# Neighbour lists from eight-column codes on TensorE, and layer 1 summed before its product

## The chip, the cores and the metric

One Trainium2 chip, one of its cores. A core has five engines that run side by side, each with its own queue, in order: TensorE (PE; its weight loads are listed as PEld), VectorE (DVE), ScalarE (ACT), GpSimd (POOL) and SyncE (SP, which only issues DMAs here). The metric is the device time of one launch in microseconds (us); lower is better. The figure of a kernel is the median of its runs.

## The reference, cut to what matters

16 graphs of 1024 nodes with 64 features go through four layers; each normalises x, applies relu, and adds its result to x. The sparse adjacency `adj` (with self loops, weights from 0.05 to 1) is the same in all of them. Layer 0 is a gated update on `A @ m`, layer 1 a normalised propagation, layer 3 a mean. Layer 2 needs the neighbours themselves: it takes out up to two neighbours of a node with many, in both directions, and then sums three quantiles of each feature over the neighbours that are left.

```python
# layer 1
norm_adj = d_inv_sqrt[:, :, None] * adj * d_inv_sqrt[:, None, :]
transformed = jnp.einsum('bnf,fu->bnu', node_features, kernel)
out = jnp.einsum('bnm,bmu->bnu', norm_adj, transformed)
# layer 2
m = nb.sum(-1)
rank = jnp.cumsum(nb, axis=-1) - 1
skip = jnp.where(m > T_THRESH, (m + K_DIL - 1) // K_DIL, 1)
do_dil = (skip > 1) & mask
removed = nb & do_dil[..., None] & ((rank + 1) % skip[..., None] == 0)
rem = removed | jnp.swapaxes(removed, 1, 2)
adj_d = jnp.where(rem, 0.0, adj_)
# then: sort the features of the neighbours of each node, channel by channel,
# and add their 0.25, 0.5 and 0.75 quantiles with weights 0.25, 0.5, 0.25
```

## The kernel before

Nodes are sorted by degree. The 128 of highest degree are the heavy rows (tile 0, in classes of capacity `HEAVY`), the other 896 the light ones (tiles 1 to 7, `LIGHT`). For each row the kernel makes a list of its neighbours, GpSimd gathers their features from a table in DRAM, and VectorE sorts them with min/max networks. The code is a set of Python generators, one for each stage and graph:

- `load` reads 128 rows of `adj` at a time (`a`), transposes them on TensorE and stores them as `adjT`; ScalarE sums the rows (`rs`).
- `ranks` makes `kx`, the column number plus one where there is a neighbour and 0 elsewhere, in fp16, stores it in DRAM as `kd`, and counts degrees with a Sign and an accumulator. Comparing the degrees gives each node its place (`sg`, `posi`). One-hot products `oh` then carry id, degree and mask of each node (`trip`) into rank order (`info`, `idn`).
- `lists` gathers the first 256 rows of `kd` in rank order (`ks2`), scans them for the rank of each neighbour, finds the one or two to be removed (`cut`), and writes zeros into `kd` at those places and their mirror images with eight scatters. It then gathers all rows again, tile by tile (`ks`), and takes the largest eight entries with MAX8, strikes them out with MATCH_REPLACE8, and repeats (`rounds`). The longest rows are cut into eight segments on the way, through `seg` and `cl` in DRAM. The lists become the indices `idxL` and `idxH`, the quantile weights `wl` and `w`.
- `dense01` is layers 0 and 1, and stores the table `tab`. `propagated` streams `adjT` through TensorE as `am`, row block by row block. Biases enter as one-row fp32 products.
- `gather_heavy` and `gather_light` issue one indirect DMA for each list position (`gh`, `s`); heavy rows pass through TensorE to put channels on partitions (`hb`). `sort_heavy`, `sort_light` and `sum_light` sort and sum; the light sorts are called 0 (tiles 1 to 3, tile `s0`) and 1 (tiles 4 to 7, `s1`). Each `s` has two buffers, `gh` six.
- `dense23` gathers the sums back to node order (`zz` from `agg`) and does the rest of layer 2 and layer 3.

The order of all instructions is fixed before the launch. The class `Order` keeps a clock for each engine from assumed durations (`Engine.duration`), and at each `yield` runs the stage that can start first; ties go to rear, sums, mid, list, rank, load, gath, sort in that order, so sorts fill what the others leave. `after(...)` holds a stage back until another has been emitted. A graph loads once the graph before has been loaded and ranked, and the graph five before has been finished (`DEPTH`). Every engine call passes through one helper line, L357, so the profile tells instructions apart by their tiles.

Of the kernel before, what the change touches and what calls it, by code (L numbers as in the profile page):

```python
# [9 lines left out]
F32 = mybir.dt.float32  # L10
# [8 lines left out]
P = 128  # L19
EPS = 1e-5  # L20
STRIP = 2
DEPTH = 5
TAUS = (0.25, 0.5, 0.75)
# [3 lines left out]
NOWHERE = 4194304.0  # L27
# [26 lines left out]
SEG_A, SEG_B, SEG_C = 26, 14, 16  # L54
USED = {1: 13, 2: 10, 3: 9, 4: 7, 5: 6, 6: 5, 7: 4}
# [123 lines left out]
class Order:  # L179
# [52 lines left out]
    def put(self, engine, us, outs, ins, landing=None, scatter=False, tail=0.0):  # L232
# [7 lines left out]
        for x in outs:  # L240
            t = max(t, self.used.get(x, 0.0), self.ready.get(x, 0.0) if scatter else 0.0)
            p = self.follows.pop(x, None)
            if p is not None:
                t = max(t, self.used.get(p, 0.0) + 0.05, self.ready.get(p, 0.0) + 0.05)
# [46 lines left out]
class Engine:  # L291
# [5 lines left out]
    def duration(self, name, outs, ins):  # L297
# [17 lines left out]
        if self.letter == "T":  # L315
            n = 1
            for _, c in list(outs[0].ap)[1:]:
                n *= c
            if name == "transpose":
                return (0.06 if ins[0].shape[0] <= 64 else 0.215), 0.17  # L320
            if two_bytes(ins[0]):
                return 0.04 + n / 2600, 0.2
            return max(0.02 + n / 510, 0.43 if ins[0].shape[1] > 64 else 0.0), 0.25
# [39 lines left out]
def kernel(  # L363
# [48 lines left out]
    onesh = const.tile([P, N], F16, name="onesh")  # L412
# [42 lines left out]
    biases = const.tile([65, 512], F32, name="biases")  # L455
    ones3 = const.tile([65, P], F32, name="ones3")
    nc.vector.memset(ones3, 1.0)
    for i, (src, n) in enumerate(((b2, H), (c2, H), (bg, 4 * H))):
        nc.sync.dma_start(biases[32 * i : 32 * i + 1, 0:n], src)
        o = biases[32 * i : 32 * i + 1, :]  # L460
        for k in range(1, 512 // n):
            nc.vector.tensor_copy(o[:, k * n : (k + 1) * n], o[:, 0:n])

    def bias(i):
        return ones3[32 * i : 32 * i + 1, :], biases[32 * i : 32 * i + 1, :]
# [7 lines left out]
    def lists_for_all():  # L473
# [9 lines left out]
        ps1 = pool("ps1", 6, space=bass.MemoryType.PSUM)  # L483
        ps2 = pool("ps2", 1, space=bass.MemoryType.PSUM)
# [29 lines left out]
        zero1 = lc.tile([P, 1], F16, name="zero1")  # L514
        nc.vector.memset(zero1, 0.0)
# [32 lines left out]
        for i in range(DEPTH):  # L548
            d = {
                "kd": dram.tile([N, N], F16, name=f"kd{i}"),  # L550
                "seg": dram.tile([32, N], F16, name=f"seg{i}"),
# [29 lines left out]
        def load(b, S):  # L581
# [8 lines left out]
            S["rs"] = rs = st.tile([P, NT], F32, name="rs")  # L590
            S["a"] = []
            for t in range(NT):
                a = ap_.tile([P, N], F32, name="a", bufs=2)
                S_.dma_start(a, adj[b, t * P : (t + 1) * P, :])
                S["a"].append(a)
                yield f"a{b}.{t}"
# [3 lines left out]
                for m in range(0, NT, 4):  # L600
# [6 lines left out]
                    ps1.close(pt)  # L607
                if t % STRIP == STRIP - 1:
                    yield "S", strip
                    S_.dma_start(  # L610
                        d["adjT"].rearrange("(m p) n -> p m n", p=P)[:, :, (t + 1 - STRIP) * P : (t + 1) * P], strip
                    )
                junk = ap_.tile([P, N], BF16, name="junk", bufs=1)
                A.activation(junk, a, AF.Copy, accum_out=rs[:, t : t + 1])
                yield after(f"b{b}.{max(0, t - 1)}")
            yield "V", rs
            V.tensor_scalar(rs, rs, 1.0, None, ALU.add)

        def ranks(b, S):

            d = D[b % DEPTH]
            yield after(f"a{b}.0")
# [3 lines left out]
            deg = ap_.tile([P, NT], F32, name="deg", bufs=2)  # L626
            for t in range(NT):
                yield after(f"a{b}.{t}")
                a = S["a"][t]
                yield "V", a  # L630
                kx = ap_.tile([P, N], F16, name="kx", bufs=2)
                V.scalar_tensor_tensor(kx, a, 0.0, iota1, ALU.is_gt, ALU.mult)
                dg = kx[:, t * P : (t + 1) * P]
                V.tensor_mul(dg, dg, offdiagh)
                yield "S", kx
                S_.dma_start(d["kd"][t * P : (t + 1) * P, :], kx)
                yield "A", kx
                junk = ap_.tile([P, N], BF16, name="junk", bufs=1)
                A.activation(junk, kx, AF.Sign, accum_out=deg[:, t : t + 1])
                yield f"b{b}.{t}"  # L640
            yield "V", deg
            trip = ap_.tile([P, NT, 3], F16, name="trip", bufs=2)
            V.tensor_scalar(trip[:, :, 0], nid, 1.0, None, ALU.add)
            V.tensor_copy(trip[:, :, 1], deg)
            V.tensor_copy(trip[:, :, 2], nm)
# [30 lines left out]

            pm = yield from bank2()
            for t in range(NT):
                yield ("V",)
                oh = ap_.tile([P, N], F16, name="oh", tag="nb", bufs=2)  # L680
                V.tensor_scalar(oh, iota1, pos1[:, t : t + 1], None, ALU.is_equal)
                yield "T", oh
                for i in range(NH):
                    sl = slice(i * 512, (i + 1) * 512)
                    T.matmul(pm[0:3, sl], trip[:, t, :], oh[:, sl], start=(t == 0), stop=(t == NT - 1))
            yield "A", pm
            byr = ap_.tile([3, N], F16, name="byr", tag="nb", bufs=2)
            A.copy(byr, pm[0:3, :])
            ps2.close(pm)
            yield "T", byr  # L690
            pb = yield from bank(F16)
            for t in range(NT):
                T.transpose(pb[:, 4 * t : 4 * t + 3], byr[:, t * P : (t + 1) * P], identh[0:3, 0:3])
            yield "V", pb
            info = ap_.tile([P, NT, 3], F32, name="info", bufs=2)
            V.tensor_copy(info, pb[:, 0 : 4 * NT].rearrange("p (t c) -> p t c", c=4)[:, :, 0:3])
            ps1.close(pb)
            idn = ap_.tile([P, NT], I32, name="idn", bufs=2)
            V.tensor_scalar(idn, info[:, :, 0], -1.0, None, ALU.add)
            S["info"], S["idn"] = info, idn  # L700

        def lists(b, S):
            d = D[b % DEPTH]
            yield after(f"rank{b}")
            info, idn = S["info"], S["idn"]

            def ranked(dst, t):
                G_.indirect_dma_start(
                    out=dst, out_offset=None, in_=d["kd"][:, :],
                    in_offset=bass.IndirectOffsetOnAxis(ap=idn[:, t : t + 1], axis=0),  # L710
                )
# [3 lines left out]
            ks2 = ap_.tile([P, 2, N], F16, name="ks2", tag="ks2")  # L715
            yield "P", idn, d["kd"]
            for t in range(2):
                ranked(ks2[:, t, :], t)
            yield "V", ks2
            inf = info[:, 0:2, :]  # L720
            half_i = ap_.tile([P, 2], I32, name="half_i", bufs=2)
            V.tensor_scalar(half_i, inf[:, :, 1], 1.0, None, ALU.add)
            V.tensor_scalar(half_i, half_i, 1, None, ALU.logical_shift_right)
            r12 = ap_.tile([P, 2, 2], F32, name="r12", bufs=2)
            V.tensor_copy(r12[:, 0, :], half_i)
            dil = ap_.tile([P, 2], F32, name="dil", bufs=2)
            V.scalar_tensor_tensor(dil, inf[:, :, 1], T_THRESH, inf[:, :, 2], ALU.is_gt, ALU.mult)
            V.tensor_mul(r12[:, 0, :], r12[:, 0, :], dil)
            V.tensor_scalar(r12[:, 1, :], r12[:, 0, :], 2.0, None, ALU.mult)
            cut = ap_.tile([P, 2, 2], F32, name="cut", bufs=2)  # L730
            for t in range(2):
                yield ("V",)
                nbk = ap_.tile([P, N], F16, name="nb", tag="nb", bufs=2)
                V.tensor_scalar(nbk, ks2[:, t, :], 1.0, None, ALU.min)
                rank = ap_.tile([P, N], F16, name="rank", tag="rank")
                V.tensor_tensor_scan(rank, onesh, nbk, 0.0, ALU.mult, ALU.add)
                for i in range(2):
                    e = ap_.tile([P, N], F16, name="e", tag="mr")
                    V.scalar_tensor_tensor(
                        e, rank, r12[:, i, t : t + 1], ks2[:, t, :], ALU.is_equal, ALU.mult,  # L740
                        accum_out=cut[:, t, i : i + 1],
                    )
                    yield ("V",)
            offi = ap_.tile([P, 2, 2, 2], I32, name="offi", bufs=2)
            none = ap_.tile([P, 2, 2], F32, name="none", bufs=2)
            V.tensor_scalar(none, cut, 0.0, NOWHERE, ALU.is_equal, ALU.mult)
            own = ap_.tile([P, 2, 2], F32, name="own", bufs=2)
            V.scalar_tensor_tensor(own, inf[:, :, 0:1].to_broadcast([P, 2, 2]), float(N), cut, ALU.mult, ALU.add)
            V.scalar_tensor_tensor(offi[:, 0], own, -float(N + 1), none, ALU.add, ALU.add)
            V.scalar_tensor_tensor(own, cut, float(N), inf[:, :, 0:1].to_broadcast([P, 2, 2]), ALU.mult, ALU.add)  # L750
            V.scalar_tensor_tensor(offi[:, 1], own, -float(N + 1), none, ALU.add, ALU.add)
            for w in range(2):
                for t in range(2):
                    for i in range(2):
                        yield "P", offi, d["kd"]
                        G_.indirect_dma_start(
                            out=d["kd"].rearrange("n (w o) -> (n w) o", o=1),
# [1093 lines left out]
```

## Time and profile before

| | us |
|---|---|
| median of 3 runs | 3383.04 (3380.87 to 3389.02) |
| the profiled execution | 3396.3 |
| its span, first to last instruction | 3394.4 |
| TensorE, mean granted clock | 0.717 of full speed |
| DMA, whole span | 489.49 MB, mean 144 GB/s |

A row of a group reads: line, engine, operation, output tile <- input tiles, sizes and type, number of instructions, then busy us and mean ns of one, then the idle us of the engine just before them and what ended most of it. Tile names lose their numbers (`s0` and `s1` are `s`, `hb0` and `hb1` are `hb`, `r12` is `r`).

### The profile page before, as it was taken

The page shows a single profiled execution, that of the slowest core. Times are in us where ns is not written, and L with a number is a line of the kernel's source. Part 1 is how long each engine was busy: PE and PEld are TensorE (multiplying, and loading weights), DVE is VectorE, ACT ScalarE, POOL GpSimd, SP SyncE. Part 2 cuts the span into 40 slices and gives each one's busy share as a digit, 9 for nine tenths or more (in the row PEclk, how much of TensorE's full clock was granted, in tenths as well). Part 3 has the DMA queues.
Part 4 walks back from the last instruction along what each step waited for, and adds up shares of the span by engine and source line. Part 5 has one row for each costly group of instructions (what it writes and reads, how often), then busy time and mean ns, then how long its engine had stood idle before and what let it go on. Part 6 is the DMA issues. An engine that isn't in the chain of part 4 may idle for free. (4 is left out here: it accounts for less than half of the span.)

```text
span 3394.4 us, 26207 instructions
## 1 busy us (share of the span) xinstructions
PE 1926.0 (57%) x5890; PEld 860.4 (25%) x5890; DVE 2895.2 (85%) x5728; ACT 1197.5 (35%) x2772; POOL 2111.6 (62%) x1839
## 2 busy tenths in 40 slices
PE   2756456727566664756666575663746566464233
PEld 1322222312223232222323223222222322221011
DVE  2355988999998999899898898989899899989992
ACT  4333343332435334143433434434243433321201
POOL 0125767565856767576674657747773776667770
PEclk9767676757767676777667677785868768577566
DMA  4445454554555465455454655454655545534222
GB/s 142 151 141 174 131 173 134 173 144 104 167 171 174 135 182 149 124 157 164 146 175 125 183 143 176 119 176 129 176 147 156 174 119 176 161 92 122 56 65 60
DMA packets 313358, 489.49 MB, mean 144 GB/s; under 512 B 127142, under 2 KB 193896, under 8 KB 313192
## 3 DMA queue, kind: packets, MB, share of 16 engines
q1 hardware_dynamic: 247144, 395.28, 36.3%
q0 software_dynamic: 66048, 92.44, 13.1%
q8 instruction: 50, 0.82, 0.1%
q14 instruction: 116, 0.95, 0.1%
HBM read 372.88 MB, written 114.63 MB: 144 GB/s over the span
## 5 line engine op out<-in xcount | busy, mean ns | idle before, releaser
L357 POOL DMA_INDIRECT s<-tab,idxL x864 | 1011.3, 1171 | 263.4 <-issue 257.6
L357 POOL DMA_INDIRECT gh<-tab,idxH x544 | 615.4, 1131 | 399.4 <-issue 186.4
L357 DVE TENSOR_TENSOR hb<-hb 128x128 f32<-128x128 f32 (+11 forms) x1072 | 741.0, 729 | 20.7 <-ACT hb L357 8.4
L357 PE MATMUL bank<-ident,a 128*128 128x128 f32 x1024 | 220.7, 375 | 379.6 <-DMA a<-in_adj_dram 359.0
L357 PE MATMUL bank<-am,tr 128*64 128x512 f32 x512 | 314.1, 754 | 173.5 <-DMA am<-adjT 167.6
L357 PE MATMUL bank<-am,hr 128*64 128x512 f32 x512 | 304.5, 733 | 123.0 <-DMA am<-adjT 87.8
L357 PE MATMUL bank<-am,m 128*64 128x512 f32 x512 | 297.8, 720 | 128.9 <-DMA am<-adjT 120.6
L357 POOL DMA_INDIRECT ks<-kd,idn x160 | 182.2, 1139 | 269.6 <-DVE idn L357 104.0
L357 POOL DMA_INDIRECT kd<-zero,offi x128 | 153.1, 1196 | 226.2 <-DVE own L357 98.5
L357 PEld LDWEIGHTS bank<-ident,a 128*128 128x128 f32 x1024 | 173.9, 196 | 434.9 <-issue 360.9
L357 DVE TENSOR_TENSOR hb<-hb,hb 128x656 f32<-128x656 f32 (+2 forms) x256 | 252.4, 1002 | 4.6
L357 ACT COPY strip<-bank 128x512 f32<-128x512 f32 x256 | 146.5, 582 | 273.9 <-PE bank L357 273.6
L357 ACT ACTIVATE junk<-kx 128x1024 bf16<-128x1024 f16 x128 | 135.3, 1057 | 295.2 <-DVE kx L357 279.6
L357 DVE SCALAR_TENSOR_TENSOR kx<-a,iota 128x1024 f16<-128x1024 f32 x128 | 156.0, 1219 | 77.6 <-DMA a<-in_adj_dram 72.0
L357 ACT ACTIVATE s<-s,wl 128x64 f32<-128x64 f32 x704 | 176.4, 336 | 59.7 <-DVE s L357 59.7
L357 POOL DMA_INDIRECT zz<-agg,posi x128 | 146.1, 1141 | 70.4 <-issue 38.4
L357 PEld LDWEIGHTS bank<-am,tr 128*64 128x64 f32 x512 | 75.8, 168 | 381.0 <-DMA am<-adjT 239.5
L357 PE MATMUL bank<-ident,gh 128*128 128x128 f32 x272 | 81.8, 352 | 142.1 <-DMA gh<-tab,idxH 141.9
L357 PE MATMUL bank<-biases,ones 1*128 1x512 f32 x192 | 147.0, 854 | 17.8 <-DVE nn L357 10.4
L357 PEld LDWEIGHTS bank<-am,hr 128*64 128x64 f32 x512 | 73.4, 163 | 311.8 <-issue 165.3
L357 PEld LDWEIGHTS bank<-am,m 128*64 128x64 f32 x512 | 72.6, 161 | 310.4 <-DMA am<-adjT 170.0
L357 ACT ACTIVATE junk<-bank,nkey 128x1024 bf16<-128x1024 f32 x128 | 142.3, 1112 | 17.5 <-PE bank L357 11.2
(227 smaller groups left out, 3732.6 us busy)
## 6 DMA issues: line engine op xcount, KB each, us to landing
am<-adjT SPq DMA_DIRECT2D x384, 512.0 KB
a<-in_adj_dram SPq DMA_DIRECT2D x128, 512.0 KB
adjT<-strip SPq DMA_DIRECT2D x64, 1024.0 KB
kd<-kx SPq DMA_DIRECT2D x128, 256.0 KB
s<-tab,idxL POOLq DMA_INDIRECT x864
gh<-tab,idxH POOLq DMA_INDIRECT x544
wb<-wd SPq DMA_DIRECT2D x32, 198.0 KB
X<-in_x_dram SPq DMA_DIRECT2D x16, 256.0 KB
```

Source lines behind the costliest of these rows:

```text
L357: return f(*args, **kw)
```

## The change

The first adjacency pass no longer makes `kx` or `kd`. ScalarE turns the transposed strip into 0/1 (`sgn`), and TensorE multiplies it with a matrix that gives each group of eight columns one code, whose bits say which of the eight are neighbours, and a count: 128 codes and 128 counts a node (`cx`). Products with the one-hots `oh`, now kept whole in SBUF, put these rows into rank order on chip. The cut is found among the 128 counts and then within one code; a second set of products carries the bits to be struck into every node's codes, which are ANDed with them and put into order again (`keys`). MAX8 searches 128 codes in place of 1024 columns; the codes found are spread to eight columns each by bit masks and searched again. Degrees come from the counts; row sums come from layer 0's propagation, which gets a column of ones (`m2x`).

Layer 1 propagates the scaled features first and multiplies with `wk` afterwards, so the transposes of `h` go. Biases enter as bf16 products of three parts. To make room, light sorts have one buffer each (`LIGHTBUFS`), `gh` four, `wb` one, and PSUM has four single and two double banks in place of six and one. `h2` is read again from `tab`. The planner's assumed durations of matmuls change.

```diff
+LIGHTBUFS = (1, 1)
+SGN = 2
+GH = 4
...
-            return max(0.02 + n / 510, 0.43 if ins[0].shape[1] > 64 else 0.0), 0.25
+                return max(0.107, 0.02 + n / 2600), 0.2
+            return max(0.02 + n / 450, 0.45 if ins[0].shape[1] > 64 else 0.0), 0.25
...
+            for k in range(512 // n):
+                nc.sync.dma_start(biases[32 * i : 32 * i + 3, k * n : (k + 1) * n], parts_d[0])
...
-        ps1 = pool("ps1", 6, space=bass.MemoryType.PSUM)
-        ps2 = pool("ps2", 1, space=bass.MemoryType.PSUM)
+        ps1 = pool("ps1", 4, space=bass.MemoryType.PSUM)
+        ps2 = pool("ps2", 2, space=bass.MemoryType.PSUM)
...
@@ load
+                S["sgn", t] = sgn = ap_.tile([P, NT, P], BF16, name="sgn", bufs=SGN)
+                A.activation(sgn, strip[:, :, o : o + P], AF.Relu)
+                A.activation(sgn, sgn, AF.Sign)
...
-                junk = ap_.tile([P, N], BF16, name="junk", bufs=1)
-                A.activation(junk, a, AF.Copy, accum_out=rs[:, t : t + 1])
...
+        def codes(b, S):
...
+                    V.tensor_mul(sgn[:, q, :], sgn[:, q, :], offdiag)
...
+                        T.matmul(
+                            pc[:, q * 256 : q * 256 + 256].rearrange("p (k o) -> p k o", k=2)[
+                                :, :, 16 * m : 16 * m + 16
+                            ],
+                            S["sgn", t + q][:, m, :], w32.rearrange("p (k o) -> p k o", k=2), start=True, stop=True,
+                        )
...
@@ ranks
-                V.scalar_tensor_tensor(kx, a, 0.0, iota1, ALU.is_gt, ALU.mult)
...
-                S_.dma_start(d["kd"][t * P : (t + 1) * P, :], kx)
...
+            if b:
+                yield after(f"masked{b - 1}")
+            S["oh"] = oh = ap_.tile([P, NT, N], F16, name="oh")
...
+                V.tensor_scalar(oh[:, t, :], iota1, pos1[:, t : t + 1], 8.0, ALU.is_equal, ALU.mult)
...
+        def permuted(oh, cx, rs, w):
...
+                T.matmul(o, ckl, ckey[:, 0:w], start=True, stop=False)
+                for t in range(NT):
+                    T.matmul(
+                        o, oh[:, t, r * P : (r + 1) * P], cx[:, t, 0:w], start=False, stop=t == NT - 1
+                    )
...
@@ lists
-                V.tensor_tensor_scan(rank, onesh, nbk, 0.0, ALU.mult, ALU.add)
...
+                V.tensor_tensor_scan(cum, onesh, cnt[:, t, :], 0.0, ALU.mult, ALU.add)
...
+                    V.tensor_scalar(oc, iota1, cut[:, 2 * t + i : 2 * t + i + 1], None, ALU.is_equal)
+                    yield "T", oc, E
+                    for n in range(NT):
+                        T.matmul(
+                            pbs[n // 4][:, n % 4 * P : (n % 4 + 1) * P], oc[:, n * P : (n + 1) * P], E[:, t, :],
+                            start=False, stop=t == i == 1 and n % 4 == 3,
+                        )
...
+                V.tensor_tensor(ci.bitcast(raw), ci.bitcast(raw), pbs[i].bitcast(raw), ALU.bitwise_and)
...
+            for rs in ((0, 1), (2, 3, 4), (5, 6, 7)):
+                yield "T", oh, cx
+                pb = yield from permuted(oh, cx, rs, w)
...
+            yield f"masked{b}"
...
+            def decoded(dst, codes, n):
...
+                V.tensor_tensor(y.bitcast(raw), k.bitcast(raw), p8.bitcast(raw), ALU.bitwise_and)
+                V.tensor_sub(dst.rearrange("p (n k) -> p n k", k=8), y, c8)
...
+            yield from rounds(4, KH, keys[:, 0, :], mk)
...
+                yield from rounds(ROUNDS[t], KL[:, COFF[t] : COFF[t] + CODES[t]], keys[:, t, :], mk)
...
+            decoded(cd, KL, NCODES)
...
@@ dense01
+            V.tensor_mul(tr, h, over_h(dinv))
             pm = yield from propagated(b, tr, own=True)
+            g0 = wp.tile([P, N], F32, name="g0", tag="big")
+            yield from evicted(pm, g0[0:H])
+            yield "T", g0
+            pm = yield from product(wk, g0[0:H])
...
@@ gather_light, gathers
-            S["s", g] = s = qp.tile([P, n * width], F32, name=f"s{g}", bufs=2)
+            S["s", g] = s = qp.tile([P, n * width], F32, name=f"s{g}", bufs=LIGHTBUFS[g])
...
-                if b >= 2:
-                    yield after(f"sum{b - 2}.{g}")
+                if b >= LIGHTBUFS[g]:
+                    yield after(f"sum{b - LIGHTBUFS[g]}.{g}")
```

## The prediction

> **What bounds it now.** I read three things first, in this order: the table of engines, the busy time by stretch, and the times at which the heavy sort of a graph hands in its sums. (A row by stretch: its bounds and length, busy us of PE, PEld, DVE, ACT and POOL with their instructions, the granted clock, DMA share and GB/s.)
>
> ```profile
> PE 1926.0 (57%) x5890; PEld 860.4 (25%) x5890; DVE 2895.2 (85%) x5728; ACT 1197.5 (35%) x2772; POOL 2111.6 (62%) x1839
> ...
> 0.00:315.00 315.00, 158.74 (x523) 78.85 (x524) 133.16 (x330) 120.17 (x226) 68.85 (x78) 0.81 0.47 148
> 500.00:3000.00 2500.00, 1510.00 (x4631) 669.83 (x4629) 2282.59 (x4489) 938.47 (x2179) 1670.46 (x1446) 0.72 0.53 153
> 3300.00:3394.00 94.00, 31.42 (x88) 13.29 (x88) 32.84 (x76) 15.47 (x52) 8.38 (x9) 0.63 0.19 56
> ...
> 455.45 1.14 SPq L357 DMA_DIRECT2D agg<-aghT  x1
> ...
> 3013.31 0.49 SPq L357 DMA_DIRECT2D agg<-aghT  x1
> ```
>
> DVE is the bound: from 500 to 3000 us it is busy 2283 of 2500 (91%). It is idle 499 us in all: 182 before the first sort at 315, 217 from 500 to 3000, 61 in the last 94, some 38 elsewhere. Between the two stores shown lie 13 graphs: 197 us a graph, of which DVE works about 180. POOL is the second bound, by its gathers and scatters (busy us, mean ns, idle us before them):
>
> ```profile
> L357 POOL DMA_INDIRECT s<-tab,idxL x864 | 1011.3, 1171 | 263.4 <-issue 257.6
> L357 POOL DMA_INDIRECT gh<-tab,idxH x544 | 615.4, 1131 | 399.4 <-issue 186.4
> ...
> L357 POOL DMA_INDIRECT ks<-kd,idn x160 | 182.2, 1139 | 269.6 <-DVE idn L357 104.0
> L357 POOL DMA_INDIRECT kd<-zero,offi x128 | 153.1, 1196 | 226.2 <-DVE own L357 98.5
> ```
>
> One takes 1.16 us, the next follows after 0.30 of issue (257.6 over 864), so 114 a graph fill 166 of the 197 us. A stage that leaves DVE is worth its DVE time until POOL or PE stands in the way.
>
> **What is removed from DVE**, by groups of DVE instructions (busy us of all 16 graphs, mean ns):
>
> ```profile
> L357 DVE SCALAR_TENSOR_TENSOR kx<-a,iota 128x1024 f16<-128x1024 f32 x128 | 156.0, 1219 | 77.6 <-DMA a<-in_adj_dram 72.0 <-issue 5.6
> L357 DVE MAX8 L<-ks 128x8 f16<-128x1024 f16 x112 | 136.7, 1222 | 0.3
> L357 DVE SCALAR_TENSOR_TENSOR e<-rank,r,ks 128x1024 f16<-128x1024 f16 x64 | 82.1, 1283 | 1.7
> L357 DVE TENSOR_TENSOR_SCAN rank<-onesh,nb 128x1024 f16<-128x1024 f16 x32 | 73.5, 2297 | 1.1
> L357 DVE MAX8 LH<-mr 128x8 f16<-128x1024 f16 x48 | 58.9, 1228 | 1.7
> ...
> L357 DVE MAX8 LA<-sg 128x8 f16<-128x128 f16 x16 | 4.5, 280 | 0.0
> L357 DVE MATCH_REPLACE8 mra<-LA,sg 128x128 f16<-128x128 f16 x16 | 4.4, 276 | 0.0
> L357 DVE TENSOR_TENSOR o<-o 128x128 f32<-128x128 f32 x16 | 4.7, 292 | 0.6
> ```
>
> The first five rows and those that go with them (busy us): kx 156.0 with its diagonal product 29.1; the rank scans 73.5, 0/1 rows 13.8, cuts 82.1 with 5.3 of accumulator reads; the searches of light rows 136.7 + 39.4 with 38.7 + 2.9 of match and replace; those of heavy rows 58.9 + 19.5, with 38.7 + 19.3 + 4.2; k0d 8.7 + 11.1; the offsets for the scatter 13.1; casts of trip, info and idn 14.8. Sum: 766 us, 48 a graph.
>
> **What is added on DVE**, a graph. The last three rows price a step on 128 columns: 0.28 for a maximum, 0.28 + 0.09 for match and replace, 0.29 for a product. 256 columns take 0.42 (hb<-hb), 512 from PSUM 0.68, 576 0.75; a column of single values 0.16 to 0.2.
> - codes: 8 diagonal products of 0.227 (the old kx row): 1.8. Casts 0.3; the one-hots multiply by 8 as well, 0.055 more at most (k0d, two operations, 544 against 489): 0.2.
> - The cut: 2 scans on 128 columns, 2297 less 896 columns at 2/0.96 ns = 0.43 each; 12 products with an accumulator, 1283 less 896/0.96 = 350, with 83 for the read, 0.43 each; 11 small steps of 0.2: 8.2.
> - Masks: 4 one-hots of 0.489, two ANDs on 512 columns, 11 steps on 128 to 256: 5.8.
> - Heavy lists: 4 maxima and 3 replacements on 128 codes (2.2), decoding on 256 (0.84), the same seven on 256 (3.2), the segments' AND and cut (1.0): 7.3.
> - Light lists: 9 maxima and 2 replacements on 128 (3.3), decoding 72 codes to 576 columns, 2 x 0.75, then 9 maxima on 128 or 64 and 2 replacements (3.0), small ones: 8.2.
>
> Sum 31.9 a graph, 510 us. Two unknowns: no row shows an AND, or a maximum over fp32. From below an AND at half a product's time (mx, 196 columns, a one-input step, 0.28) and accumulators at 0.29 give 450. From above, maxima and replacements at twice the slope of the fp16 rows add 0.13 on each of some 37, and ANDs at a scan's 2 columns a cycle 3: 640. I take 510, since MAX8 at 1222 ns for 1024 two-byte columns runs one column a cycle, with no two-byte gain to lose. Net on DVE: **-256 us** (-126 to -316).
>
> **Waits on DVE.** From 500 to 3000 us, waits of 57 us go with their instructions: k0d on ks 28.8, nm on its DMA 17.3 (now long loaded), kx 5.0, info and oh 5.8. New ones come: the ranking now passes between PE, ACT and DVE some ten times more a graph (cnt, k01, two mask banks, three permuted banks, sg2 by DMA, m0). The nearest row is this wait, in us in all, times and longest:
>
> ```profile
> DVE nn L357 <- ACT rz L357: 61.2, 17, 7.5
> ```
>
> Over some 26 such hand-overs in that stretch it is 2.4 us each. Most hand-overs find a sort to fill them: I take two of the ten, +60 over 13 graphs (one 30, six or seven 200).
>
> **Start and end.** The first heavy gather waits at 235.6 us for nz, but the table it reads is only stored at 214.9, by layer 1, whose length the change hardly touches. So the lists of graph 0, which lose their DMA trips through kd, gain at most 20; 18 more DMAs for the bias parts stand on SP ahead of the first load, at the 0.25 to 0.6 us of its neighbours, with three round trips: some 10 back. -10 (-40 to +30). At the end only sorts are left: 100 us of DVE a graph, while POOL needs 96 x 1.46 = 140. Already now POOL is busy 233 of 300 us there; with one light buffer in place of two it can't run ahead: +20 (0 to 60).
>
> **POOL, buffers, ACT, DMA.** 160 gathers of ks and 128 scatters go (335 us busy, 26 a graph with issue): POOL then needs 140 of 180. One light buffer: the gather of 32 (47 us) starts after the sum of the graph before (8.4 us of scaling on ACT, adds, a store: 20) and must land before the same sort of the next graph, that is within the other light sort and the heavy sort, 78 us of DVE or some 128 with the other work between: covered. Without that cover 67 us a graph would lie open. ACT loses 407 (row sums, degrees, k0p, byr, hT) and gains about 506, 271 of it two passes over each sgn tile at 1.06: 1300, hidden. 65 MB less pass for kd, 8% of DMA's load.
>
> **PE** loses 88 (oh,trip), 107 of the 147 of bias products, 70 for hT and wk. It gains 49 (wk after the sum) and 3008 small products (1024 codes, 1440 permutations, 544 masks) with 128 transposes of 30 in all. Rows of small two-byte products go from 161 ns (byr) to 291 (drT,sel). At 0.16 to 0.2 by width that is 534 more: net +348, and the 118 a graph of 500 to 3000 us become 140; at 0.29, net +686, 161. Behind it stand waits for am, 22 a graph, and for gh, 7: 169 to 190 against 180. It is hidden, just.
> The Trainium skill, TensorE: Matmul & The Clock Gate, section Back-to-back issue gap, gives a sustained 81 ns for a pair of weight load and 128-column matmul at the full clock. By it the small products would come to 244 us, PE would stay near 120 a graph and out of the way. The rows here, at a granted clock of 0.72, are two to three times that, and contain the drain of a lone product.
>
> **The sum.** Profiled span 3394, less 256, less 57, plus 60, less 10, plus 20: 3151. The profiled run's time was 3396.3, 2 above its span, and 13 above the median 3383: **3140**.
>
> **Rivals.**
> A. PE becomes the bound: at 161 a graph and 29 of waits, in order, a propagation that waits for am holds up codes and permutations. At 190 us a graph: 445 + 13 x 190 + 367 (the end as it is, less the DVE gain, plus 20) = 3282, less 11: 3270. For it: PE waits 376 us for am. Against: some of the modelled busy time is overlap.
> B. Everything fits better: DVE's new waits at 30, the start at -40, no loss at the end: 3394 - 256 - 57 + 30 - 40 = 3071, so 3060; with DVE's lower price 3000.
> C. Slower: light gathers with one buffer. POOL's order is fixed (heavy, light 0, light 1 of a graph, then the next), so when light 0 waits for a sum, the heavy gathers behind it wait too, with four gh tiles in place of six (POOL waits 115 us for gh's transposes already with six). The loop over two graphs is 47 + 32 + 50 of gathers, 107 + 36 of sorts with work between, 20 of sum: 292, with waits 310, that is 155 a graph. It decides from 180, and makes the kernel slower from 197, a gather of about 2 us in place of 1.46. At 205: 455 + 13 x 205 + 381 = 3501, so 3490. Against: undisturbed gathers here take 0.95.
> D. The DVE time is saved and all of it comes back as idle time, with other work ready too late: 3383.
>
> **Chances.** Forecast, 3060 to 3230: 0.50. B 0.17. A 0.19, of which 0.18 still faster and 0.01 the same. C 0.11. D 0.03, of which 0.02 same and 0.01 slower. A measurement of this kernel tells 0.3% (10 us; its three runs lie 8 apart) from no change. Faster 0.85, same 0.03, slower 0.12. The range goes from B's low end to above A: 2990 to 3350.
>
> **What would show it.** DVE busy near 2640, share 83 to 85%; 13 graphs at about 180 us between the stores of aghT; no kd on any queue; POOL at 1776 busy; PE at 2050 to 2450. AND and MAX8 rows on fp32 at the prices above are right, at twice them wrong. It is wrong if DVE's idle time passes 600 us, with DVE s or hb waiting for gathers (C) or for PE's pb (A), or if DVE's busy time stays above 2770.

## The result and the profile after

The changed kernel takes 3491.7 us (median of 4 runs, 3487.7 to 3498.2) beside 3385.6 for the kernel before on the same chip: a ratio of 1.032, 95% interval 1.029 to 1.034. The forecast was 3140, faster; it is slower. The span of the profiled execution is 3492.5 us.

The table of engines and the busy time by stretch (columns as in the prediction):

```profile
PE 1875.0 (54%) x8258; PEld 916.3 (26%) x8258; DVE 2608.5 (75%) x6678; ACT 1273.1 (36%) x3138; POOL 1678.1 (48%) x1553
```

```profile
0.00:315.00 315.00, 188.42 (x988) 102.75 (x988) 161.54 (x636) 158.24 (x319) 74.18 (x81) 0.79 0.49 149
500.00:3000.00 2500.00, 1377.47 (x6074) 668.28 (x6074) 1931.06 (x4881) 933.83 (x2318) 1235.32 (x1146) 0.73 0.44 124
```

VectorE did lose its work: 2895.2 us have become 2608.5, 287 less where 256 were forecast. But it now stands still: in the middle stretch it is busy 77% of the time in place of 91%, and its idle time over the span went from 499 to 884 us. The heavy sums follow one another more slowly:

```profile
375.35 0.50 SPq L368 DMA_DIRECT2D agg<-aghT  x1
...
3113.80 0.50 SPq L368 DMA_DIRECT2D agg<-aghT  x1
```

That is 13 graphs of 210.6 us (before: 196.8; forecast: 180). Two lists of waits, VectorE's and POOL's (what waited, for what, us in all, times, longest):

```profile
DVE zz L368 <- DMA zz<-agg,posi: 497.8, 16, 50.5
```

```profile
POOL gh L368 <- PE bank L368: 371.1, 101, 26.8
POOL s L368 <- ACT s L368: 266.7, 7, 69.7
...
POOL s L368 <- DVE oh L368: 112.8, 3, 54.3
```

VectorE waits once a graph, for some 31 us, for the gathers that bring the sums back to node order (`zz`). POOL waits once a graph ahead of a light gather: all such waits over 2.5 us make 627 us in 15 times. All 15 lie ahead of the first gather into `s0`, which starts 2.5 to 6.9 us behind the store of the sum that empties this buffer; the releaser that the profile names differs from graph to graph. Before the change no such wait was longer than 0.3 us:

```profile
POOL s L357 <- issue: 257.6, 845, 0.3
```

One graph of POOL, VectorE and SP's stores, by the timeline (start, length, engine, what, and in brackets the idle time before):

```profile
1483.63 0.94 POOL L368 DMA_INDIRECT gh<-tab,idxH  x1 [0.30 <-issue]
1540.27 0.94 POOL L368 DMA_INDIRECT s<-tab,idxL  x1 [55.69 <-ACT s L368]
...
1600.79 0.94 POOL L368 DMA_INDIRECT zz<-agg,posi  x1 [0.30 <-issue]
```

```profile
1612.06 0.69 DVE L368 TENSOR_TENSOR zz<-zz,h2r 128x512 f32<-128x512 f32 x1 [41.10 <-DMA zz<-agg,posi]
```

```profile
1536.40 0.38 SPq L368 DMA_DIRECT2D agg<-s  x1
...
1711.48 0.50 SPq L368 DMA_DIRECT2D agg<-aghT  x1
1744.42 0.38 SPq L368 DMA_DIRECT2D agg<-s  x1
```

Read it as a ring. The sum of light sort 0 is stored at 1536.4; only then may the next graph's gathers write into the one buffer `s0`, and POOL, whose queue is in order and has this gather next, has stood 56 us. 46 light gathers take 60 us; the `zz` gathers of the graph before stand behind them in the queue, and VectorE, whose queue has the `zz` addition in the middle of the next heavy sort, stands 41 us. The sort ends at 1711.5, the light sort's sum is stored at 1744.4, and the ring closes after 208 us: 3.9 to the first gather, 60.5 of gathers, 11.3 of `zz`, 99.4 to the heavy sums, 32.9 to the light ones. The chain that ended last goes round it:

```profile
DVE 43%; POOL 18%; PE 11%; DMA 9%; issue 9%; ACT 7%; SPq 1%; DVEq 0%; POOLq 0%; ACTq 0%
```

### The profile page after: what moved, and what is told of

Read it like the earlier page. It is cut to its first block, busy times and chain, and to the rows that moved or that the text cites. A ratio compares the mean times of both kernels' runs of the same rounds, so it can differ in the third digit from the quotient of the medians.

```text
span 3492.5 us, 31295 instructions
## 1 busy us (share of the span) xinstructions
PE 1875.0 (54%) x8258; PEld 916.3 (26%) x8258; DVE 2608.5 (75%) x6678; ACT 1273.1 (36%) x3138; POOL 1678.1 (48%) x1553
## 4 chain that ended last, share of the span: by engine, by line
DVE 43%; POOL 18%; PE 11%; DMA 9%; issue 9%; ACT 7%; SPq 1%; DVEq 0%; POOLq 0%; ACTq 0%
DVE hb L368 18%; POOL s L368 16%; PE bank L368 11%; DMA am<-adjT 5%; DVE s L368 4%; POOL zz L368 3%; DVE o L368 2%; ACT junk L368 2%; DMA zz<-agg,posi 2%; DMA a<-in_adj_dram 1%; ACT s L368 1%; SPq L368 1%; ACT sgn L368 1%; DVE KH L368 1%; DVE ln_s L368 1%
## 5 line engine op out<-in xcount | busy, mean ns | idle before, releaser
L368 POOL DMA_INDIRECT s<-tab,idxL x864 | 962.3, 1114 | 887.4 <-ACT s L368 266.7
L368 POOL DMA_INDIRECT gh<-tab,idxH x544 | 587.9, 1081 | 793.8 <-PE bank L368 371.1
L368 PE MATMUL bank<-am,tr 128*64 128x512 f32 x512 | 294.9, 712 | 152.5 <-DMA am<-adjT 72.2
L368 PE MATMUL bank<-ident,zz 128*64 128x128 f32 x128 | 31.7, 407 | 607.2 <-DMA s<-tab,idxL 372.6
L368 PE MATMUL bank<-am,m2x 128*65 128x512 f32 x512 | 297.0, 716 | 94.4 <-DMA am<-adjT 84.3
L368 PEld LDWEIGHTS bank<-ident,a 128*128 128x128 f32 x1024 | 152.2, 178 | 213.7 <-issue 125.3
L368 POOL DMA_INDIRECT zz<-agg,posi x128 | 123.3, 963 | 68.0 <-issue 35.7
L368 PE MATMUL bank<-cx,oh 128*128 128x133 f16 (+1 forms) x1280 | 140.9, 259 | 15.4 <-ACT cx L368 11.0
L368 DVE TENSOR_TENSOR s<-s,o 128x576 f32<-128x576 f32 (+5 forms) x256 | 137.6, 552 | 5.2
L368 PEld LDWEIGHTS bank<-am,m2x 128*65 128x65 f32 x512 | 76.0, 165 | 246.1 <-issue 123.0
```

Of the source, the lines that this page charges most:

```text
L368: return f(*args, **kw)
```

## Where the order comes from

Why would the program queue light gathers so far ahead of their buffer? The order is fixed by the class `Order`, and its own clocks say when it believed each thing to happen. In three successive graphs it starts the gathers into `s0` at 1083, 1252 and 1416 us and the store that releases `s0` at 1138, 1302 and 1461: some 50 us too early each time (over all 15 graphs that follow another, 11 to 76 us ahead of the landing of that store). It has a rule for a reused buffer, the note `follows`, but it takes the note away with the first instruction that writes the tile (`self.follows.pop(x, None)`). For a light tile that is a padding copy on ScalarE (`far`); the gathers after it are planned as if the buffer were free. With two buffers a gather is never that early (in the plan of the kernel before, 133 us or more behind the landing), so the gap in the rule cost nothing. The plan's own end went from 3225 to 2948 us, while the chip went from 3394 to 3492.

Theory 1: the plan is blind to the release of the only light buffer, and the queues it fixes make a ring. Rivals: the single buffer itself (2), the change's new prices in the plan (3). The recorded expectations number them a little differently: in runs 1 to 4 theory 3 is TensorE's extra work, and in run 5 theory 2 is a lucky other order.

## Experiments

Ratios are to the kernel before, run on the same chip in the same set. Runs 1 to 4, 9 to 12, 17 and 18 had it at 3381 to 3390 us and stand together; 5 to 8 and 13 to 16 fell on two other chips, where it took 3542 and 3552, and come last.

**1. The plan keeps the note.**

```diff
-            p = self.follows.pop(x, None)
+            p = self.follows.get(x)
```

> The changed kernel, with the planner alone altered: every writer of a tile, not just the first, is planned to wait until the tile before it in the same buffer has been read. Theory 1 (blind plan): a light tile is written first by ScalarE's padding copies, which take the note of the old tile away, so the plan starts gathers into the one buffer some 50 us before its last data are stored; on the chip POOL waits there, the gathers of zz stand behind those of s, and DVE stands at the addition of zz. Then DVE's waits at zz fall from 498 us to under 150 and the time to 3100 to 3250. Theory 2 (buffers): one light buffer starves the sorts in whatever order; then waits for gathers take the place of those at zz and the time stays above 3400. Theory 3 (TensorE's extra work) expects no change over 1%.

> The kernel of the first experiment once more, as the link between two sets of runs: where the second four ran, the kernel before itself took 3542 us in place of 3386, and their traces hold waits on events of which the profile doesn't know the sender, so that they are not to be set beside the first four. Theory 1 (one light buffer and a plan that doesn't see its release): ratio to before 0.88 to 0.92 again. Theory 4 (a kernel with so many instructions or hand-overs loses on such a chip whatever its plan): ratio over 1.0 where before takes 3540.

3030.2 us, ratio 0.896 (0.892 to 0.899), and once more in run 9, as the link to a later set: 3030.5, 0.894 (0.890 to 0.899). That is less than theory 1 expected (3100 to 3250); theory 2 (above 3400) and TensorE's extra work (no change over 1%) fall. Not an instruction of the computation differs, only the order; but the edit keeps the note for every tile of the program, and run 11 tests the light ones alone. Its engines and middle stretch:

```profile
PE 1884.9 (62%) x8258; PEld 925.1 (31%) x8258; DVE 2611.7 (86%) x6678; ACT 1283.7 (42%) x3144; POOL 1750.1 (58%) x1553
```

```profile
500.00:2800.00 2300.00, 1508.68 (x6473) 727.66 (x6471) 2141.12 (x5326) 986.97 (x2459) 1450.29 (x1278) 0.76 0.50 144
```

VectorE is busy 93% there. POOL still starts its light gathers just behind the store, but has gathered heavy rows until then:

```profile
1511.93 1.16 POOL L368 DMA_INDIRECT gh<-tab,idxH  x1 [0.30 <-issue]
1515.87 0.95 POOL L368 DMA_INDIRECT s<-tab,idxL  x1 [2.79 <-ACT strip L368]
...
1556.35 1.48 POOL L368 DMA_INDIRECT zz<-agg,posi  x1 [3.55 <-DMA agg<-s]
```

```profile
1513.08 0.37 SPq L368 DMA_DIRECT2D agg<-s  x1
```

The `zz` gathers now go in among the light ones, and VectorE's waits at `zz` are two, 33 us in all:

```profile
DVE zz L368 <- DMA zz<-agg,posi: 33.1, 2, 19.0
```

The plan's own end, 3010, is now near the chip's 3032.

**2. Only the addition of `zz` later in VectorE's queue**, plan as blind as before:

```diff
+            order.ready[zz.tensor.name] += 45.0
             yield "V", zz
```

> The changed kernel, with the addition of zz planned 45 us later on DVE; buffers and the blind plan stay. Theory 1: DVE no longer stands at zz (under 150 us of 498), sorts go on meanwhile, 3200 to 3350. Theory 2: the same idle time at sorts waiting for gathers, within 1% of 3492. Theory 3: within 1%.

3482.5, ratio 1.029 (1.025 to 1.033). Theory 1's number was missed by far; "within 1% of 3492", which theories 2 and 3 had, came true, though VectorE doesn't stand at sorts waiting for gathers as theory 2 has it. The wait at `zz` fell from 498 to 35 us as meant, and the time came back elsewhere; POOL's and VectorE's waits:

```profile
DVE zz L368 <- DMA zz<-agg,posi: 35.4, 3, 12.3
...
POOL s L368 <- ACT s L368: 613.4, 11, 83.2
...
DVE sgn L368 <- ACT sgn L368: 210.9, 20, 50.8
...
DVE oc L368 <- PE bank L368: 82.2, 5, 43.0
```

POOL now stands 795 us ahead of light gathers in place of 627, again 15 times and each time at `s0`, 2.5 to 4.6 us behind the store. The largest wait of VectorE was a symptom: without it a graph still takes 208.7 us, and the ring closes on the same buffer.

**3 and 4. One light buffer in the kernel before**, with its plan blind and seeing:

```diff
-            S["s", g] = s = qp.tile([P, n * width], F32, name=f"s{g}", bufs=2)
+            S["s", g] = s = qp.tile([P, n * width], F32, name=f"s{g}", bufs=1)
...
-                if b >= 2:
-                    yield after(f"sum{b - 2}.{g}")
+                if b >= 1:
+                    yield after(f"sum{b - 1}.{g}")
```

> The kernel before with one buffer for each light sort in place of two and nothing else. Theory 1: the same waits at zz appear, 200 to 500 us, time 3550 to 3750. Theory 2: slower too, by 100 to 300, with waits at s or hb for gathers. Theory 3: within 1% of 3386.

> As the one before, with the planner altered as in the first. Theory 1: most of the loss comes back, 3390 to 3450, waits at zz under 100. Theory 2: as slow as with the blind plan, within 1%.

Blind 3489.1, ratio 1.031 (1.027 to 1.035); seeing 3423.2, 1.012 (1.008 to 1.016). The sign is as theory 1 expected, the size not: 103 us, which is what theory 2 had (100 to 300), and VectorE waits only 42 us at `zz`. POOL stands only 115 us for the buffer in run 3; by the clocks of its own plan the gathers into `s0` start just 1 to 24 us ahead of the landing that they need, in the changed kernel 11 to 76. Run 4 is as theory 1 expected (3390 to 3450; theory 2 had it as slow as run 3): two thirds of the loss goes when the plan sees, and 37 us are left with one buffer each.

**10 and 18. Two buffers for `s0`**, blind and seeing:

```diff
-LIGHTBUFS = (1, 1)
+LIGHTBUFS = (2, 1)
...
-                    strip = ap_.tile([P, NT, STRIP * P], F32, name="strip", bufs=2)
+                    strip = ap_.tile([P, NT, STRIP * P], F32, name="strip", bufs=1)
...
-                    oc = ap_.tile([P, N], F16, name="oc", bufs=2)
+                    oc = ap_.tile([P, N], F16, name="oc", bufs=1)
```

> The blind plan with two buffers for the large light sort (strips and cut one-hots with one), beside the link. Theory 1: a ratio within 0.03 of the link's. Theory 2 (the loss is not in the buffer): as the changed kernel, 1.03.

> Two buffers for the large light sort and a plan that sees the release. Beside a kernel before at 3386 to 3390: 3030 to 3110 if one light buffer costs nothing once the plan knows of it (and the 3293 of the blind plan with these buffers was the blindness to the other one), 2920 to 3000 if it costs much. Beside some 3550: 3555 again.

Blind 3292.6, ratio 0.972 (0.967 to 0.977); seeing 3073.5, 0.909 (0.907 to 0.911). The first misses what theory 1 expected (0.86 to 0.92), and its profile says why: the stand has moved to the other light sort, whose buffer is still the only one. SP's stores and POOL's gathers of run 10, `s0` from 1393.0, `s1` from 1507.0:

```profile
1393.02 1.16 POOL L368 DMA_INDIRECT s<-tab,idxL  x1 [0.30 <-issue]
...
1507.02 1.34 POOL L368 DMA_INDIRECT s<-tab,idxL  x1 [69.80 <-DMA agg<-s]
```

```profile
1504.21 0.38 SPq L368 DMA_DIRECT2D agg<-s  x1
```

The expected number left `s1` out; the plan of this kernel starts `s1`'s gathers at 1315 and stores the sum that releases it at 1382. Seeing the release is worth 219 us with these buffers. And a second buffer for `s0` alone gains nothing once the plan sees: 3073 with it, 3030 without (the single strip and `oc` that pay for it may cost some of these 43; that was not measured by itself). It doesn't show that single buffers are free: in run 18 POOL still stands 13 times ahead of `s1`, 293 us in all, and two buffers for both sorts were never run in the changed kernel.

**11. Padding behind the gathers**, so that a gather is the first writer; `Order` untouched:

```diff
             S["s", g] = s = qp.tile([P, n * width], F32, name=f"s{g}", bufs=LIGHTBUFS[g])
-            far(s, g, 0)
...
                     gather(b, keys[:, j, at], S["idxL"][:, OFFS[t] + j : OFFS[t] + j + 1])
                     yield ("P",)
+            far(s, g, 0)
```

> Padding copies behind the gathers, plan otherwise blind, beside the link. Its own plan ends 108 us later than the link's (3118 to 3010), as the sort now waits for copies that ScalarE's queue holds behind the gathers. Theory 1: 60 to 160 us over the link, so a ratio of 0.91 to 0.95, with POOL's wait for the buffer gone. Theory 2: 1.0 or more.

3099.6, ratio 0.915 (0.911 to 0.919): as theory 1 expected, except that POOL's wait for the buffer is not gone. No padding lies ahead of the gathers here, and those that wait still start 2.5 to 8.5 us behind the store, so it is the buffer and not the padding copy that they wait for. Two edits that share nothing but the note each take away more than half of POOL's stand (627 us to 261 here, to 151 in run 1), and end 2% apart. A lucky order is hardly left as a rival.

**17. The change's other edits to the plan undone**, plan blind:

```diff
-            t = max(t, self.used.get(x, 0.0) + 0.035, self.ready.get(x, 0.0) if scatter else 0.0)
+            t = max(t, self.used.get(x, 0.0), self.ready.get(x, 0.0) if scatter else 0.0)
...
-                return max(0.107, 0.02 + n / 2600), 0.2
-            return max(0.02 + n / 450, 0.45 if ins[0].shape[1] > 64 else 0.0), 0.25
+                return 0.04 + n / 2600, 0.2
+            return max(0.02 + n / 510, 0.43 if ins[0].shape[1] > 64 else 0.0), 0.25
```

> The other edits to the plan undone, the note of the buffer blind. Beside a kernel before at 3386 to 3390 us (undisturbed): theory 1: 3430 to 3600; theory 3 (the new prices make the plan a bad one): 3050 to 3250. Beside a kernel before at some 3550: 4033 again, and nothing new.

3751.9, ratio 1.109 (1.105 to 1.113). Theory 3 falls, with the opposite sign: the new prices, with the 0.035 us that the change adds after a tile's last use, save 260 us in the blind plan. Theory 1 had expected less of a loss, but the place is its own:

```profile
POOL s L368 <- ACT s L368: 938.3, 13, 115.2
```

**12. Prices nearer to the measured ones** (VectorE `(cols + 74) / 845`, a gather 1.30), two buffers as in run 18, plan seeing.

> Two buffers, a plan that sees the release, prices nearer to those measured, beside the link. If the order of work still costs something in the link: 20 to 70 us less than it. If the rest is VectorE's own work: within 15 us of it.

3154.9, ratio 0.932 (0.927 to 0.936): 124 us more than run 9 and 81 more than run 18. Neither number came true. Totals nearer to the truth made a worse order; POOL stands 465 us at `s`, all of it at `s1`. The kernel of run 1 stays the best version, faster than both.

The runs side by side. "At s" is POOL's idle time ahead of light gathers, waits over 2.5 us, with their number:

| kernel | buffers s0, s1 | plan | at s, us | DVE idle, us | time, us |
|---|---|---|---|---|---|
| before | 2, 2 | blind | 0 | 499 | 3386 |
| after | 1, 1 | blind | 627 (15) | 884 | 3492 |
| 2 | 1, 1 | blind, zz later | 795 (15) | 875 | 3483 |
| 17 | 1, 1 | blind, old prices | 1093 (15) | 1136 | 3752 |
| 10 | 2, 1 | blind | 455 (11) | 684 | 3293 |
| 11 | 1, 1 | note kept by a gather | 261 (8) | 483 | 3100 |
| 12 | 2, 1 | sees, other prices | 465 (13) | 539 | 3155 |
| 18 | 2, 1 | sees | 293 (13) | 458 | 3073 |
| 1 | 1, 1 | sees | 151 (9) | 420 | 3030 |

VectorE's work is the same to 8 us in all rows but the first, so its idle time is the time. In each of the pairs that differ in the note alone the plan that sees is the faster: 3492 to 3030, 3293 to 3073, and 3489 to 3423 in the kernel before with one buffer. That is what theory 1 says. What a single buffer costs by itself, in a plan that sees it, stays open.

**5 to 8 and 13 to 16, on two other chips.** Run 5 is the kernel of 11, 6 and 13 that of 17, 7 that of 10, 8 that of 12, 15 that of 18; 14 adds the edit of run 1 to that of 17, and 16 has the edit of run 1 with six `gh` tiles and one strip.

> The changed kernel with nothing but the order of two steps of a light gather swapped: ScalarE's padding copies into s are issued behind the gathers instead of ahead of them, so that a gather is the first writer of the buffer and the plan's note of the buffer's last tile goes to it. The plan is otherwise as blind as in the changed kernel. Theory 1 (the plan puts light gathers ahead of the release of the only buffer, and POOL stands there): the program's own plan now ends at 3118 us in place of 2948 and has no gather ahead of its release; on the chip 3090 to 3190, POOL's wait for s under 30 us a graph. Theory 2 (the earlier repair helped by a lucky other order, not because of the buffer): near 3490, or anywhere without the wait having gone.

> The changed kernel with the plan's prices as before (two-byte matmuls 0.04 + n/2600, fp32 ones n/510, no 0.035 after the last use of an output): the change's other edits to the plan undone, the note of the buffer as blind as it was. Theory 1: the light gathers are still planned some 60 us ahead of the release, 3440 to 3530. Theory 3 (the new prices of matmuls make the plan a bad one): 3050 to 3250.

> The changed kernel with two buffers for the large light sort (s0), paid for with one buffer in place of two for the transposed strips and for the one-hots of the cuts; the plan is left blind. Theory 1: with two buffers a blind plan no longer puts a gather ahead of its release, so 3000 to 3100, with POOL's wait for s gone; and what it lies below 3030 is what one buffer costs by itself. If the strips need their second buffer, DVE's or ACT's waits for strip show it and it is up to 60 longer. Theory 2 (the loss is not in the buffers): 3400 to 3500.

> As the run before it, but with a plan that sees the buffer's release and prices nearer to what the profile shows (VectorE's instructions 14% longer: 2612 us measured in all against 2296 planned; a gather 1.30 in place of 1.43). Meant as the best version. If the order of work still costs something: 2960 to 3010. If the repaired kernel is bound by VectorE alone (2612 busy, 420 idle of which 250 lie at start and end): 3010 to 3040, no more to be had by planning.

> The change's other edits to the plan undone (prices of matmuls as before, no 0.035 after the last use), the note of the buffer as blind as in the changed kernel; tried once where the traces were disturbed, so once more. Its own plan ends at 2979 us and puts light gathers some 60 us ahead of the release. Theory 1 (one light buffer and a plan that doesn't see its release): ratio 1.01 to 1.06. Theory 3 (the new prices make the plan a bad one): 0.90 to 0.96.

> The same with the plan that sees the release; its own plan ends at 3032. Theory 1: 0.89 to 0.92. Theory 3: below 0.89. If it and the run before it lie within 0.02, the blindness isn't the cause.

> Two buffers for the large light sort, one for strips and for the one-hots of the cuts, plan sees the release; its own plan ends at 3051. What one light buffer costs once the plan knows of it: if much, 0.86 to 0.885 (2920 to 3000); if nothing, 0.89 to 0.915, and the 0.972 of the blind plan with these buffers then lies in the blindness to the other light sort's only buffer, for which POOL stood 60 to 70 us a graph.

> Plan sees the release, and six tiles for the heavy gathers in place of four (one buffer for the strips pays); its own plan ends at 3086. In the repaired kernel POOL waits 404 us for the transposes that free these tiles. If that is on the path: 0.87 to 0.885 and the wait under 200. If VectorE alone bounds it: 0.89 to 0.92, with the wait gone elsewhere.

They took, in order, 3780, 4036, 3655 and 3659 beside 3542 (ratios 1.064, 1.139, 1.029, 1.033), and 4033, 3566, 3555 and 3612 beside 3552 (1.135, 1.005, 1.000; the four runs of the last lie between 3514 and 3663, too far apart for a ratio). None of the numbers expected for them came true there; the theory 4 of run 9 (such a kernel loses on these chips whatever its plan) fits runs 14 and 15. What they have in common with the others: on one chip, the edit of run 1 takes the old-price kernel from 4033 to 3566. What they show for themselves is that the gain over the kernel before is not there on these chips. In their traces engines stand on events whose sender the profile doesn't know. In run 5 POOL's stand at `s` is that of run 11, the same kernel (262 and 261 us), but its span is 679 us longer, and VectorE stands 374 us on such events, in run 11 not at all. VectorE's waits in run 5, and one such place on PE and VectorE:

```profile
DVE y L368 <- remote: 121.5, 3, 67.3
...
DVE m L368 <- remote: 50.2, 2, 32.3
```

```profile
983.53 0.19 PE L368 MATMUL bank<-c,bsel 128*128 128x1 f16 x2 [4.95 <-issue]
```

```profile
1012.63 0.21 DVE L368 SCALAR_TENSOR_TENSOR m<-rowl,cs,bank 128x1 f32<-128x1 f32 x1 [32.35 <-remote]
```

The product that `m` reads was done at 984, VectorE reads it at 1013, and nothing recorded lies between. Why, stays open; the kernel of run 1 itself never ran on such a chip, and whether six `gh` tiles help can't be said from run 16.

## Why the prediction was wrong, step by step

- **VectorE's sum: right.** 287 us saved against 256. The two unknowns came out at the value taken: an AND costs what a product does (680 ns for 512 columns with one operand in PSUM, 751 for 576, against 0.68 and 0.75 taken), and MAX8 over fp32 what it does over fp16 (278 ns for 128 columns, against 280). The upper bound calls the scan "2 columns a cycle", which is the wrong way round: at 2297 ns for 1024 columns it is the slower one, a product of that width taking 1218 (groups by form of the kernel after: busy us, mean ns):

```profile
L368 DVE TENSOR_TENSOR codes<-codes,bank 128x512 int32<-128x512 int32 x32 | 21.6, 680 | 2.8 <-ACT s L368 1.6 <-PE bank L368 1.1
...
L368 DVE TENSOR_TENSOR y<-KL,dpow 128x576 int32<-128x576 int32 x16 | 12.0, 751 | 0.0
```

```profile
L368 DVE MAX8 KL<-keys 128x8 f32<-128x128 f32 x112 | 26.1, 278 | 0.0
```

- **POOL, buffers: the step that failed.** "The gather of 32 (47 us) starts after the sum of the graph before … and must land before the same sort of the next graph … covered." The sentence counts durations, and these held: light gathers took 1114 ns on average, less than before. What it left out is that queues are in order and that the order had been fixed by a plan which didn't know of the wait. The room of 128 us exists only if other work stands in it in POOL's and VectorE's queues; here nothing stood in POOL's (56 us idle) and the `zz` gathers stood behind. The blind plan makes 210.6 us a graph of it. Run 1 gives the forecast's own kernel, with the work arranged as that sentence assumed: 176.8 us a graph over 13 graphs, where 180 were forecast:

```profile
375.53 0.50 SPq L368 DMA_DIRECT2D agg<-aghT  x1
...
2673.69 0.50 SPq L368 DMA_DIRECT2D agg<-aghT  x1
```

- **Rival C named the place, but its number is luck.** One light buffer with POOL's queue held up behind it is where the time went, and VectorE's idle time passed the 600 us that were its sign (884). That its 3490 lies beside 3492 is luck: its 205 us a graph stood for a gather of some 2 us, and gathers took 1.32 us from start to start (60.5 for 46). Nor did VectorE wait at `s` or `hb` for gathers, as the sign has it (its longest wait there is 2.9 us, for ScalarE); it waited at `zz`, which C's loop doesn't hold. A loop of durations leaves out what the queues have put into it: `zz` in POOL's, the rest of the heavy sort behind `zz` in VectorE's. At 0.11 it had too small a chance.
- **Waits on DVE: right in kind, too dear.** With the order repaired, VectorE's idle time is 420 us where the forecast's terms left 512 (3151 less 2639). Ten more hand-overs a graph cost little, and the end gained: from the store of the fourteenth heavy sums on it takes 358 us (2673.69 to 3031.6), before 381.
- **The start: mis-sized, and it hid part of the loss.** Forecast -10 (-40 to +30). The first heavy gather starts 45 us sooner (first line before the change, second after), and the first heavy sums are stored 80 us sooner (375.35, before 455.45):

```profile
235.59 0.94 POOL L357 DMA_INDIRECT gh<-tab,idxH  x1 [16.47 <-DVE nz L357]
```

```profile
190.55 1.11 POOL L368 DMA_INDIRECT gh<-tab,idxH  x1 [174.10 <-DVE ln_v L368]
```

  The prediction took the store of the table, at 214.9, as the limit and as hardly touched. It came at 186.8, and `nz`, for which the gather had waited, is ready before it. Why the table comes 28 us sooner no run tests. With the plan repaired the forecast would have been too long by 110 us (3140 for 3030), some 70 of them here: the sum has the first heavy sums at 445, run 1 at 375.5.
- **PE: mis-sized, without effect.** Forecast +348, measured -51. I multiplied counts by the mean time of one product (161 to 291 ns). The records of successive products overlap: 1024 of 247 ns keep PE busy for only 97.3 us. Busy time over count is the price:

```profile
L368 PE MATMUL bank<-cx,oh 128*128 128x133 f16 x1024 | 97.3, 247 | 11.0 <-ACT cx L368 11.0
...
L368 PE MATMUL bank<-E,oc 128*128 128x128 f16 x512 | 54.5, 273 | 76.7 <-DVE oc L368 76.4 <-issue 0.2
L368 PE MATMUL bank<-w,sgn 128*128 128x32 bf16 x1024 | 47.7, 181 | 118.7 <-DVE sgn L368 85.8 <-ACT sgn L368 32.6
```

  95, 106 and 47 ns each, not 247, 273 and 181. All 3008 small products came to 295 us in place of 534 (these three groups with 43.7 for 256 columns and 52.0 for the two-row ones). With 295 the sum would have read +109. The rest of the way to -51 lies in products that the change left alone (the three propagations take 882 us after 916, the transposes of `a` 204 after 221) and in more overlap between groups. The Trainium skill (TensorE: Matmul & The Clock Gate, Back-to-back issue gap) has 81 ns sustained for a product of 128 columns in a stream with its weight loads, by which these products come to an estimated 244 us: much nearer than 534, at a mean granted clock of 0.73 here. PE's busy time fell, so rival A had nothing behind it.

## What to carry to other kernels

Where a program fixes the order of in-order queues from its own model, a cut in buffers is first a question to that model: does it know when the buffer comes free, for every writer of the tile and not just the first? Compare the model's own end with the chip's; here a plan that got faster (2948 from 3225) while the chip got slower had lost sight of a dependency. The two blind plans with one buffer end at 2948 and 2979 (run 17) for spans of 3492 and 3745, those that keep the note at 3010, 3051 and 3118 (runs 1, 18 and 11) for 3032, 3070 and 3093. And a wait that moves when its place in the queue is changed, as `zz` did, was a symptom: look for the ring, and for the resource that it closes on.

## What the hardware showed beyond that

- The same instructions in another order took 3030 or 3752 us: order alone was worth 24%.
- A gather on POOL, while the other engines stand, takes 0.94 us and the next starts 0.30 after it, for dozens in a row; the mean of light gathers is lower where VectorE stands longer: 1184 ns in run 1 (420 us idle), 1114 in the changed kernel (884), 1067 in run 17 (1136). A falling mean can be a sign of waiting.
- On two of the chips the kernel before took 5% longer (3542 and 3552 to 3386), and the kernel of run 18 took 16% longer (3555 to 3073), with VectorE's busy time unchanged (2612 and 2614 us).
